# Four GNN layers on one core: layer 0's group boundary reordered, its evictions on two engines, one bias sum and one row transform moved

## The chip, the cores and the metric

The kernel runs on one core of a Trainium2 chip. The metric is the device time of one execution in microseconds (us); lower is better. Five engines work side by side, each through its own queue of instructions: TensorE (PE) multiplies matrices and writes PSUM, VectorE (DVE) and ScalarE (ACT) do elementwise work, GpSimd (POOL) does elementwise work on SBUF, and SyncE (SP) issues transfers. ACT and POOL issue transfers as well. Engines wait for each other by semaphores, which the tile framework sets.

## The reference, cut to what matters

There are N = 2708 nodes with 512 features, an int32 adjacency matrix of 0 and 1 (2708 x 2708), and four layers. Each is `x = x + layer(relu(layernorm(x)))`:

```python
# layer 0:  h = relu(layernorm(x))
out = (adj.T @ h) @ W0
x = x + relu(out * clip(adj.sum(axis=0), 1)[:, None] ** -0.5)
# layer 1:  keep = the first 64 neighbours of each row, by a running count along the row
x = x + leaky(h @ W_line.T + b_line) + leaky(mean(keep @ h) @ W_nb.T + b_nb)
# layer 2:  8 heads of graph attention, e = leaky(f1[:, None] + f2[None, :], 0.2), softmax over neighbours
x = x + elu(attention @ Wh)
# layer 3:  mean over neighbours and self, each through a weight, then both through W_comb
x = x + relu(concat(self, nb) @ W_comb + b_comb)
```

## The kernel before

Rows are cut into NC = 22 chunks of R = 126 (the last has 62), and chunks of columns into six groups of 4, 4, 4, 4, 3 and 3. Layer 0 multiplies by the weight first (`h0 = h @ W0`, split into two parts whose sum is exact enough, `halves`), then by the adjacency.

**Layer 0** (lines 350 to 462) runs over 132 units (group g, row chunk m). `staged` writes the steps of several units one behind the other: `load0` of unit i, the layer norm and product of chunk i (for the first 22 units alone), `count0` of unit i-3 and `multiply0` of unit i-4. This is the order of priority only. The framework's scheduler sets the final order within each engine's queue from a model of time, so an operation may stand some units ahead of its place.

- `load0` fetches a block of the adjacency (`ai`, three buffers).
- `count0`: VectorE casts it to `ar` for the products (line 381); ScalarE squares it into `ab`, a bf16 copy (line 383); VectorE scans along the row (line 388), which gives the running count `cum`; POOL keeps its last column in `deg` (line 396); ScalarE takes the sign of 64 minus the count, in place over `cum`, with the row sum into `signs` (line 397).
- `multiply0`: PE adds this unit's products to the group's 4 (or 3) accumulators (line 306), then transposes `ab` by multiplying with a unit matrix that has two columns of ones more (line 421), which also gives the column sums. ScalarE copies the transpose to `vT`, int8, which layers 1 to 3 read (line 424); VectorE takes the column sums out of the same PSUM tile (line 425). All PSUM tiles come from one pool of eight.
- After a group's last unit `finish0` sums the columns (line 439), takes 1/sqrt (lines 440 to 444), and for each chunk k of the group evicts the accumulator with relu and scale on ScalarE (line 449) into `y`, adds it to x on POOL (line 450), and writes x1 to memory, a transfer that the ScalarE queue issues (line 97). `y` and the layer norm's `hn` share three buffers (tag `t`).

**Ahead of layer 0** (lines 247 to 287) W_self and W_nb of layer 3 are each multiplied with their half of W_comb, and the biases too: eight matmuls with a broadcast bias column (line 279), then one addition on VectorE (line 286).

**Layer 2** first computes Wh = h W, f1 and f2 by chunk (lines 566 to 595). `row2` transposes f1 of a chunk to a row and copies it into `rows_T` (8 heads x 2772). After all chunks one Exp runs over `rows_T` (line 598), one transfer writes it to memory (`rT`, line 599), and each head's loop begins by loading its row, repeated on 126 partitions (`rb`, line 691). The loop scales it on ScalarE (`t`, line 702), combines it with the mask on VectorE (line 705) and multiplies on PE (line 715).

`load_x` (line 235) loads a chunk of x into a ring of seven buffers that all layers share. Weights of the layers take turns in two buffers (tag `w`).

Of the kernel before, what the change touches and what calls it, by code (L numbers as in the profile page):

```python
# [8 lines left out]
F32 = mybir.dt.float32  # L9
F32R = mybir.dt.float32r  # L10
BF16 = mybir.dt.bfloat16
I32 = mybir.dt.int32
# [30 lines left out]
def fast_layers(  # L43
# [188 lines left out]
            )  # L232
        return t

    def load_x(src, c, name="x", pool=None, bufs=7, twice=False):
        n = rows(c)
        t = (pool or common).tile([P, D], F32, name=name, bufs=bufs)
        if twice and c == NC - 1:
            nc.gpsimd.memset(t[:R], 0.0)
            move(nc.sync, t[TAIL : TAIL + n, :], src[c * R : c * R + n, :])  # L240
        move(nc.sync, t[:n], src[c * R : c * R + n, :])
        return t
# [4 lines left out]
    with tc.tile_pool(name="pre", bufs=2) as pre:  # L247
        ws = [load_weight(pre, w_self, "ws")]
        wc = load_weight(pre, w_comb, "wc", k=2 * NF)
        ws.append(load_weight(pre, w_nb3, "ws"))  # L250
        bc = load_row(pre, b_comb, "bc")
        bcol = pre.tile([P, 2 * NF], F32, name="bcol")
        for i, b in enumerate((b_self, b_nb3)):
            nc.sync.dma_start(
                bcol[:, i * NF : (i + 1) * NF], b.rearrange("(k p) -> p k", p=P)
            )
        for i in range(2):
            wsT = pre.tile([P, NF, D], F32, name="wsT")
            for f in range(NF):
                pt = ps.tile([P, NF, P], F32, name="wsT_ps", tag="ps")  # L260
                for k in range(NF):
                    nc.tensor.transpose(pt[:, k, :], ws[i][:, f, k * P : (k + 1) * P], ident)
                nc.scalar.copy(wsT[:, :, f * P : (f + 1) * P], pt)
            wf = pre.tile([P, NF, D], F32, name="wf")
            for f in range(NF):
                po = ps.tile([P, D], F32, name="fused_ps", tag="ps")
                for k in range(NF):
                    nc.tensor.matmul(
                        po,
                        wsT[:, k, f * P : (f + 1) * P],  # L270
                        wc[:, i * NF + k, :],
                        start=(k == 0),
                        stop=(k == NF - 1),
                    )
                nc.vector.tensor_copy(wf[:, f, :], po)
            nc.gpsimd.dma_start(fused[i].rearrange("(k p) o -> p k o", p=P), wf)
        pb = ps.tile([P, D], F32, name="bias3_ps", tag="ps")
        for k in range(2 * NF):
            nc.tensor.matmul(
                pb,  # L280
                bcol[:, k : k + 1].to_broadcast([P, P]),
                wc[:, k, :],
                start=(k == 0),
                stop=(k == 2 * NF - 1),
            )
        nc.vector.tensor_tensor(bc, pb, bc, ALU.add)
        nc.gpsimd.dma_start(bias3, bc[:1])

    vpool = ctx.enter_context(tc.tile_pool(name="vpool", bufs=1))
# [60 lines left out]
    with ExitStack() as ring_ctx:  # L350
        ring = ring_ctx.enter_context(tc.tile_pool(name="ring", bufs=NC - 1))

        w0s = load_weight(weights, w0, "w0s", tag="w")
        h0 = {}

        def product0(c, xc, hT, n):
            po = ps.tile([P, D], F32, name="h0_ps", tag="ps")
# [3 lines left out]
        with tc.tile_pool(name="l0", bufs=2) as wk:  # L361
# [2 lines left out]

            def load0(i):
                g, m = units[i]
                cs, n, gw = groups[g], rows(m), width(groups[g])
                ai = wk.tile([R, WG], I32, name="ai", bufs=3)
                block = adj[m * R : m * R + n, cs[0] * R : cs[0] * R + gw]
                if m == NC - 1:  # L370
                    nc.gpsimd.memset(ai[:, :gw], 0)
# [4 lines left out]
            def count0(i):  # L376
# [8 lines left out]
                if gw < KR:  # L385
# [21 lines left out]
            def multiply0(i):  # L407
# [4 lines left out]
                if m == 0:  # L412
                    for c in cs:
                        acc[c] = ps.tile([P, D], F32, name="acc", tag="ps")
                    sums[g] = wk.tile([R, KMAX, NC], F32, name="sums")
                for k, c in enumerate(cs):
                    matmuls(acc[c], h0[m], ar, k, m)

                pt = ps.tile([P, KMAX, P], F32, name="vT_ps", tag="ps")
                for k in range(K):  # L420
                    nc.tensor.matmul(
                        pt[:, k, :], ab[:n, k * R : k * R + P], ident1[:n], start=True, stop=True
                    )
                nc.scalar.copy(vT[g][:, :, m * R : (m + 1) * R], pt[:R, :K, :R])
                nc.vector.tensor_copy(
                    sums[g][:, :K, m : m + 1], pt[:R, :K, R : R + 1]
                )
                if m == NC // 2:
                    xs.update((c, load_x(x_in, c)) for c in cs)
                if m == NC - 1:  # L430
                    finish0(g)

            def finish0(g):
                cs = groups[g]
                K = len(cs)

                nc.gpsimd.memset(vT[g][:, :, N:], 1)
                nrm = small.tile([R, KMAX], F32, name="nrm")
                nc.vector.tensor_reduce(ind[:R, cs[0] : cs[-1] + 1], sums[g][:, :K], AX.X, ALU.add)
                nc.vector.tensor_scalar(  # L440
                    nrm[:, :K], ind[:R, cs[0] : cs[-1] + 1], 1.0, None, op0=ALU.max
                )
                nc.scalar.activation(nrm[:, :K], nrm[:, :K], AF.Sqrt)
                nc.vector.reciprocal(nrm[:, :K], nrm[:, :K])
                for k, c in enumerate(cs):
                    n = rows(c)
                    xc = xs.pop(c)
                    r = common.tile([P, D], F32, name="y", tag="t", bufs=3)
                    nc.scalar.activation(r[:n], acc.pop(c)[:n], AF.Relu, scale=nrm[:n, k : k + 1])
# [99 lines left out]
    with tc.tile_pool(name="l2", bufs=1) as cp:  # L549
# [13 lines left out]
        rows_T = pp.tile([H, NC * R], F32, name="rows_T", bufs=1)  # L563
        if N < NC * R:
            nc.gpsimd.memset(rows_T[:, N:], 0.0)
# [32 lines left out]
        nc.scalar.activation(rows_T[:, :N], rows_T[:, :N], AF.Exp, scale=1.0 - SLOPE2)  # L598
# [87 lines left out]
        for cs in spans:  # L686
            W = len(cs) * R
            for hd in range(H):
# [705 lines left out]
```

## Time and profile before

The time is 2215.93 us, the median of 3 runs (2213.86 to 2220.64). The profiled execution spans 2214.2 us. Its stages, by the lines that start in them and by the busy time of each engine in these stretches:

| stretch, us | what runs | PE busy | DVE busy | ACT busy | mean PE clock |
|---|---|---|---|---|---|
| 0 to 196 | fused weights, bias; dense part and group 0 of layer 0 | 178.62 | 90.70 | 75.89 | 0.98 |
| 196 to 248 | layer 0, group 1 | 49.16 | 34.87 | 37.22 | 0.96 |
| 248 to 308 | group 2 | 52.51 | 39.12 | 43.12 | 0.89 |
| 308 to 364 | group 3 | 49.77 | 37.62 | 41.07 | 0.94 |
| 364 to 413 | group 4 (3 chunks) | 39.40 | 30.43 | 34.86 | 0.90 |
| 413 to 458 | group 5 (3 chunks) | 39.65 | 30.59 | 32.59 | 0.89 |
| 560 to 760 | a part of layer 1 | 200.00 | 106.24 | 12.02 | 1.00 |
| 1000 to 1820 | layer 2, attention | 816.31 | 675.87 | 584.41 | 1.00 |
| 1820 to 2215 | layer 3 | 385.33 | 133.78 | 33.56 | 0.99 |

PE's busy time counts a matmul at half clock as busy too, so a stretch with a mean clock under 1 holds a second loss beside the idle time. The page's chain of waits names by line what ended last; the timeline lists instructions in order of time with the wait ahead of each, in square brackets, and what released it.

### The profile page before, as it was taken

The numbers are of one execution on the slowest core, as the hardware profiler recorded it, in microseconds if no ns is written. First come the engines' busy times: TensorE is split into PE (matmuls) and PEld (weight loads), VectorE is DVE, ScalarE is ACT, GpSimd is POOL, SyncE is SP. The second block draws the span as 40 slices with busy tenths as digits, with TensorE's granted clock in tenths as the row PEclk, the third lists the DMA queues.
The fourth block names the chain that finished last, engine by engine and source line by source line (L and its number), as shares of the span: only waits on it lengthen the run. The fifth ranks groups of instructions, "written<-read, shape, count | busy, mean of one in ns | idle before, by whom it ended". The sixth has DMA issues, their size and how long they took to land.

```text
span 2214.2 us, 21084 instructions
## 1 busy us (share of the span) xinstructions
PE 2116.3 (96%) x7176; PEld 1111.1 (50%) x7176; DVE 1379.4 (62%) x2137; ACT 972.4 (44%) x1489; POOL 244.2 (11%) x420
## 2 busy tenths in 40 slices
PE   8998888889999998879999999999999999999998
PEld 4555666644468875423333333333333334448886
DVE  4455666754446566658888888787888873323343
ACT  2445677741100001347777776666777762210000
POOL 1001232221102111310000000000001100000000
PEclk9999899999999999989999999999999999999999
DMA  6224444422221212010110201010100103211131
GB/s 236 70 75 125 131 139 125 114 81 71 71 77 52 62 43 93 31 45 25 25 33 26 60 28 28 28 28 24 35 25 24 31 9 93 67 57 57 57 106 34
DMA packets 117893, 140.64 MB, mean 64 GB/s; under 512 B 56784, under 2 KB 73404, under 8 KB 117768
## 3 DMA queue, kind: packets, MB, share of 16 engines
q1 hardware_dynamic: 80024, 103.82, 16.2%
q10 hardware_dynamic: 37176, 33.28, 4.8%
q0 software_dynamic: 576, 2.10, 0.3%
q8 instruction: 58, 0.95, 0.2%
q14 instruction: 59, 0.48, 0.1%
HBM read 103.54 MB, written 35.46 MB: 63 GB/s over the span
## 4 chain that ended last, share of the span: by engine, by line
PE 56%; ACT 1%; DMA 0%; DVE 0%; issue 0%; POOL 0%; DVEq 0%; ACTq 0%; SPq 0%
PE att L715 37%; PE acc L306 10%; PE nb_ps L165 3%; PE self_ps L165 3%; PE wh_ps L165 1%; ACT ot L649 1%; PE hT_ps L186 1%; PE out_ps L652 0%; DMA rb<-rT 0%; DMA rT<-rows_T 0%; DVE f L580 0%; ACT rows_T L598 0%; ACT t L702 0%; POOL wh_a L574 0%; DVE x L760 0%
## 5 line engine op out<-in xcount | busy, mean ns | idle before, releaser
L715 PE MATMUL att<-t,wh 126*65 126x504 f32 (+2 forms) x2112 | 828.5, 553 | 11.6 <-DVE t L705 11.6
L705 DVE SCALAR_TENSOR_TENSOR t<-t,eg,vT 126x882 f32<-126x882 f32 (+3 forms) x528 | 633.7, 1213 | 150.6 <-ACT t L702 149.1
L702 ACT ACTIVATE t<-rb,ef 126x882 f32<-126x882 f32 (+3 forms) x528 | 556.8, 1064 | 243.4 <-PE att L715 190.6
L715 PEld LDWEIGHTS att<-t,wh 126*65 126x65 f32 (+1 forms) x2112 | 287.7, 138 | 536.4 <-issue 449.5
L306 PE MATMUL acc<-halves,kt 126*126 126x512 f32 x1848 | 432.7, 395 | 1.2 <-DVE kt L522 1.2
L306 PEld LDWEIGHTS acc<-halves,kt 126*126 126x126 f32 x1848 | 343.8, 186 | 88.1 <-DVE kt L522 2.9
L306 PE MATMUL acc<-halves,ar 126*126 126x512 f32 x924 | 268.0, 431 | 22.2 <-DVE ar L381 12.9
L306 PEld LDWEIGHTS acc<-halves,ar 126*126 126x126 f32 x924 | 172.2, 197 | 72.2 <-DVE ar L381 14.5
L174 ACT ACTIVATE ln_rs<-ln_mv,eps 126x1 f32<-126x1 f32 x88 | 25.3, 293 | 319.5 <-DVE ln_mv L172 317.1
L522 DVE SCALAR_TENSOR_TENSOR kt<-lastr,index,vT 126x504 fp32r<-126x504 int16 (+1 forms) x132 | 104.3, 798 | 80.4 <-PE acc L306 79.7
L683 POOL TENSOR_TENSOR xs<-xs,e 126x448 f32<-126x448 f32 (+3 forms) x32 | 53.9, 1695 | 815.4 <-DVE e L669 815.4
L748 DVE CAST kt<-vT 126x504 fp32r<-126x504 int8 (+1 forms) x132 | 52.7, 400 | 144.8 <-PE acc L306 140.8
L388 DVE TENSOR_TENSOR_SCAN cum<-ai,deg 126x504 int16<-126x504 int32 (+2 forms) x110 | 125.9, 1146 | 25.7 <-DMA ai<-in_adj 15.4
L397 ACT ACTIVATE cum<-cum,limit 126x504 int16<-126x504 int16 (+3 forms) x132 | 88.1, 668 | 106.4 <-POOL ab L384 73.0
L188 ACT ACTIVATE hT<-hT_ps 128x504 f32<-128x504 f32 x88 | 51.1, 586 | 156.7 <-PE hT_ps L186 134.1
L170 DVE BATCH_NORM_STATS2 ln_st<-x 126x6 f32<-126x512 f32 x88 | 60.1, 686 | 85.0 <-DMA x<-x 65.4
L165 PE MATMUL wh_ps<-w2s,hT 128*126 128x512 f32 (+1 forms) x176 | 82.3, 611 | 7.8 <-ACT hT L188 7.8
L383 ACT ACTIVATE ab<-ai 126x504 bf16<-126x504 int32 (+3 forms) x132 | 76.7, 581 | 14.6 <-DMA ai<-in_adj 14.4
L165 PE MATMUL nb_ps<-wn,hT 128*126 128x512 f32 x176 | 81.5, 606 | 1.3 <-ACT hT L188 1.3
L165 PE MATMUL h_ps<-w0s,hT 128*126 128x512 f32 x176 | 79.3, 593 | 0.2 <-ACT hT L188 0.2
L165 PE MATMUL nb_ps<-wfn,hT 128*126 128x512 f32 x176 | 79.3, 593 | 0.2 <-ACT hT L188 0.2
L165 PE MATMUL line_ps<-wl,hT 128*126 128x512 f32 x176 | 79.1, 592 | 0.0
(132 smaller groups left out, 1503.8 us busy)
## 6 DMA issues: line engine op xcount, KB each, us to landing
x<-x SPq DMA_DIRECT2D x105, 252.0 KB
ai<-in_adj SPq DMA_DIRECT2D x84, 248.1 KB
x<-x ACTq DMA_DIRECT2D x63, 252.0 KB
x<-in_x SPq DMA_DIRECT2D x42, 252.0 KB
rb<-rT SPq DMA_DIRECT2D x16, 434.1 KB
s<-y ACTq DMA_DIRECT2D x21, 252.0 KB
sc<-s SPq DMA_DIRECT2D x21, 252.0 KB
out_x<-x ACTq DMA_DIRECT2D x21, 252.0 KB
```

What stands on the lines that cost most here:

```text
L165: nc.tensor.matmul(po[:n], lhsT[:, f, :n], w[:, f, :], start=(f == 0), stop=(f == NF - 1))
L170: nc.vector.bn_stats(st[:n], xc[:n])
L306: nc.tensor.matmul(acc[:R], weight[:, k * R : (k + 1) * R], parts[:, i, :], start=(m == 0 and i == 0), stop=(m == NC - 1),)
L383: nc.scalar.activation(ab[:n, :gw], ai[:n, :gw], AF.Square)
L388: nc.vector.tensor_tensor_scan(cum[:n, :gw], ai[:n, :gw], ai[:n, :gw], 0.0 if g == 0 else deg[:n, m : m + 1], op0=ALU.add, op1=ALU.max,)
L397: nc.scalar.activation(cum[:n, :gw], cum[:n, :gw], AF.Sign, bias=limit[:n], scale=-1.0, accum_out=signs[:n, m, g : g + 1],)
L522: nc.vector.scalar_tensor_tensor(by_chunk(kt, cs), lastr[:, cs[0] * R : (cs[-1] + 1) * R].rearrange("p (c r) -> p c r", r=R), index[:R, m ...
L683: nc.gpsimd.tensor_tensor(xs[:n, :q], xs[:n, :q], e[:n, k : k + q], ALU.add)
L702: nc.scalar.activation(t[:n, :W], rb[:n, :W], AF.Copy, scale=ef[:n, m, hd : hd + 1])
L705: nc.vector.scalar_tensor_tensor(by_chunk(t, cs)[:n], by_chunk(t, cs)[:n], eg[:n, m, hd : hd + 1], pattern(m, cs, n), op0=ALU.max, op1=ALU ...
L715: nc.tensor.matmul(a[:O1, : hi - lo], wh[:n, m, hd, :], t[:n, lo:hi], start=(m == 0), stop=(m == NC - 1),)
L748: nc.vector.tensor_copy(by_chunk(kt, cs), pattern(m, cs))
```

## The change

It has six parts. (1) In the last unit of a group the transposes and the column sums come ahead of the products, and the normalizing factor is computed before them. (2) Odd chunks are evicted on VectorE (`max` with 0, then times the factor), even ones on ScalarE as before. (3) The sign is written to a tile of its own (`sign`, bf16, one buffer), and in every unit the column sums (VectorE) stand ahead of the copy to `vT` (ScalarE). (4) `ai` has four buffers, and the x ring six. (5) The bias sum is formed on VectorE, by eight fused multiply-adds over 128 partitions, and one matmul with ones sums the partitions. (6) Layer 2's f1 row is written to memory by chunk from a small tile, the transfer issued by ScalarE, and the Exp moves to after the load of `rb`, on 126 partitions. The weights of layer 1 are asked for at unit 44 of layer 0, and not after it.

The purpose: the factor is to be ready when the products end, so that the accumulators are freed soon; the evictions are to share two engines; the sign need not wait until POOL has read the count; PE gets rid of seven bias matmuls; and the attention can start without one Exp and one transfer over all rows.

```diff
-    def load_x(src, c, name="x", pool=None, bufs=7, twice=False):
+    def load_x(src, c, name="x", pool=None, bufs=6, twice=False):
...
+        part = pre.tile([P, D], F32, name="part", bufs=1)
+        nc.vector.tensor_scalar(part, wc[:, 0, :], bcol[:, 0:1], None, op0=ALU.mult)
+        for k in range(1, 2 * NF):
+            nc.vector.scalar_tensor_tensor(
+                part, wc[:, k, :], bcol[:, k : k + 1], part, op0=ALU.mult, op1=ALU.add
+            )
         pb = ps.tile([P, D], F32, name="bias3_ps", tag="ps")
-        for k in range(2 * NF):
-            nc.tensor.matmul(
-                pb,
-                bcol[:, k : k + 1].to_broadcast([P, P]),
-                wc[:, k, :],
...
-        nc.vector.tensor_tensor(bc, pb, bc, ALU.add)
+        nc.tensor.matmul(pb[:1], ones, part, start=True, stop=True)
+        nc.vector.tensor_tensor(bc[:1], pb[:1], bc[:1], ALU.add)
...
+                if i == 2 * NC:
+                    l1_weights.extend(
+                        load_weight(weights, w, name, tag="w")
+                        for w, name in ((w_nb1T, "wn"), (w_line1T, "wl"))
+                    )
...
-                ai = wk.tile([R, WG], I32, name="ai", bufs=3)
+                ai = wk.tile([R, WG], I32, name="ai", bufs=4)
...
+                sign = wk.tile([R, WG], BF16, name="sign", bufs=1)
                 nc.scalar.activation(
-                    cum[:n, :gw],
+                    sign[:n, :gw],
                     cum[:n, :gw],
                     AF.Sign,
...
-                for k, c in enumerate(cs):
-                    matmuls(acc[c], h0[m], ar, k, m)
+                def products():
+                    for k, c in enumerate(cs):
+                        matmuls(acc[c], h0[m], ar, k, m)
+
+                if m < NC - 1:
+                    products()
 
                 pt = ps.tile([P, KMAX, P], F32, name="vT_ps", tag="ps")
                 for k in range(K):
                     nc.tensor.matmul(
                         pt[:, k, :], ab[:n, k * R : k * R + P], ident1[:n], start=True, stop=True
                     )
+                nc.vector.tensor_copy(sums[g][:, :K, m : m + 1], pt[:R, :K, R : R + 1])
+                if m == NC - 1:
+                    nrm = small.tile([R, KMAX], F32, name="nrm")
+                    total = ind[:R, cs[0] : cs[-1] + 1]
+                    nc.vector.tensor_reduce(total, sums[g][:, :K], AX.X, ALU.add)
+                    nc.vector.tensor_scalar(nrm[:, :K], total, 1.0, None, op0=ALU.max)
+                    nc.scalar.activation(nrm[:, :K], nrm[:, :K], AF.Sqrt)
+                    nc.vector.reciprocal(nrm[:, :K], nrm[:, :K])
+                    products()
                 nc.scalar.copy(vT[g][:, :, m * R : (m + 1) * R], pt[:R, :K, :R])
-                nc.vector.tensor_copy(
-                    sums[g][:, :K, m : m + 1], pt[:R, :K, R : R + 1]
-                )
...
-                    nc.scalar.activation(r[:n], acc.pop(c)[:n], AF.Relu, scale=nrm[:n, k : k + 1])
+                    if k % 2:
+                        nc.vector.tensor_scalar(
+                            r[:n],
+                            acc.pop(c)[:n],
+                            0.0,
+                            nrm[:n, k : k + 1],
+                            op0=ALU.max,
+                            op1=ALU.mult,
+                        )
+                    else:
+                        nc.scalar.activation(
+                            r[:n], acc.pop(c)[:n], AF.Relu, scale=nrm[:n, k : k + 1]
+                        )
...
-        wl = load_weight(weights, w_line1T, "wl", tag="w")
-        wn = load_weight(weights, w_nb1T, "wn", tag="w")
...
+        wn, wl = l1_weights
...
-            nc.tensor.transpose(pf[:H, :n], f12[:n, c, :H], ident[:n, :n])
-            nc.scalar.copy(rows_T[:, c * R : c * R + n], pf[:H, :n])
+            nc.tensor.transpose(pf[:H], f12[:R, c, :H], ident[:R, :R])
+            row = pp.tile([H, R], F32, name="row")
+            nc.scalar.copy(row, pf[:H])
+            nc.scalar.dma_start(rT[:, c * R : (c + 1) * R], row)
...
-        nc.scalar.activation(rows_T[:, :N], rows_T[:, :N], AF.Exp, scale=1.0 - SLOPE2)
-        nc.sync.dma_start(rT, rows_T)
...
+                nc.scalar.activation(rb[:, :W], rb[:, :W], AF.Exp, scale=1.0 - SLOPE2)
```

More of the change, by code (lines that the diff above doesn't have):

```diff
@@ L276, in fast_layers @@
             nc.gpsimd.dma_start(fused[i].rearrange("(k p) o -> p k o", p=P), wf)
-        pb = ps.tile([P, D], F32, name="bias3_ps", tag="ps")
-        for k in range(2 * NF):
-            nc.tensor.matmul(
-                pb,
-                bcol[:, k : k + 1].to_broadcast([P, P]),
-                wc[:, k, :],
-                start=(k == 0),
-                stop=(k == 2 * NF - 1),
-            )
-        nc.vector.tensor_tensor(bc, pb, bc, ALU.add)
+        part = pre.tile([P, D], F32, name="part", bufs=1)
[4 more added lines that the diff above has]
+            )
+        pb = ps.tile([P, D], F32, name="bias3_ps", tag="ps")
+        nc.tensor.matmul(pb[:1], ones, part, start=True, stop=True)
+        nc.vector.tensor_tensor(bc[:1], pb[:1], bc[:1], ALU.add)
         nc.gpsimd.dma_start(bias3, bc[:1])
@@ L354, in fast_layers @@
         h0 = {}
+        l1_weights = []
         def product0(c, xc, hT, n):
@@ L423, in multiply0 @@
                     )
+                nc.vector.tensor_copy(sums[g][:, :K, m : m + 1], pt[:R, :K, R : R + 1])
[7 more added lines that the diff above has]
+                    products()
                 nc.scalar.copy(vT[g][:, :, m * R : (m + 1) * R], pt[:R, :K, :R])
-                nc.vector.tensor_copy(
-                    sums[g][:, :K, m : m + 1], pt[:R, :K, R : R + 1]
-                )
                 if m == NC // 2:
                     xs.update((c, load_x(x_in, c)) for c in cs)
[L430 to L435, printed above, removed]
-                nc.gpsimd.memset(vT[g][:, :, N:], 1)
[L438 to L444, printed above, removed]
+                if m < NC - 1:
+                    return
+                nc.gpsimd.memset(vT[g][:, :, N:], 1)
                 for k, c in enumerate(cs):
@@ L562, in fast_layers @@
             )
-        rows_T = pp.tile([H, NC * R], F32, name="rows_T", bufs=1)
-        if N < NC * R:
-            nc.gpsimd.memset(rows_T[:, N:], 0.0)
         def product2(c, xc, hT, n):
```

## The prediction

> **What bounds the kernel now.** I read the page first: busy shares, then slices.
>
> ```profile
> PE 2116.3 (96%) x7176; PEld 1111.1 (50%) x7176; DVE 1379.4 (62%) x2137; ACT 972.4 (44%) x1489; POOL 244.2 (11%) x420
> ...
> PE   8998888889999998879999999999999999999998
> ...
> PEclk9999899999999999989999999999999999999999
> ```
>
> PE is the bound, busy for 96%. Work taken off another engine counts only where PE waits for it, and PE is idle for 2214.2 - 2116.3 = 97.9 us in all. The slices put the idle time in the first quarter (layer 0) and in slices 16 to 18 (layer 2's dense part and the entry to its attention); the attention has almost none. Next, PE's waits in 0 to 480 us (us in total, times, longest):
>
> ```profile
> PE acc L306 <- DVE ar L381: 13.6, 7, 3.9
> PE vT_ps L421 <- ACT ab L383: 13.2, 11, 2.1
> PE acc L306 <- DVE halves L227: 5.1, 8, 0.8
> ...
> PE acc L306 <- DVE sums L425: 4.2, 4, 2.1
> ...
> PE acc L306 <- DVE tail L230: 3.3, 1, 3.3
> ```
>
> Groups 1 to 5 own the first two rows. In an undisturbed stretch of the timeline a unit takes 2.155 us with 4 chunks, 1.634 with 3, so 22 units take about 46.7 and 35.5 us. The groups' first products stand at 196.5, 248.4, 308.3, 364.0 and 413.5, and the last transposes end at 457.9: they take 52.0, 59.9, 55.7, 49.5 and 44.4. The **boundary loss** is 5.3 + 13.2 + 9.0 + 14.0 + 8.9 = 50.4 us. The timeline from group 1 to group 2 shows how it arises (start, duration, engine, instruction, wait ahead of it):
>
> ```profile
> 247.78 0.39 PE L421 MATMUL vT_ps<-ident,ab 62*128 62x128 bf16 x4
> ...
> 251.86 0.56 ACT L424 CAST vT<-vT_ps 126x504 int8<-126x504 f32 x1
> ...
> 253.18 0.14 DVE L425 COPY sums<-vT_ps 126x4 f32<-126x4 f32 x1
> ...
> 254.07 0.18 DVE L444 RECIPROCAL nrm<-nrm 126x4 f32<-126x4 f32 x1 [0.27 <-ACT nrm L443]
> ...
> 254.64 1.82 ACT L449 ACTIVATE y<-acc,nrm 126x512 f32<-126x512 f32 x3
> ...
> 258.18 4.10 ACTq L97 DMA_DIRECT2D x<-x  x3
> ...
> 263.37 0.63 ACT L383 ACTIVATE ab<-ai 126x504 bf16<-126x504 int32 x1
> ...
> 264.06 0.40 PE L421 MATMUL vT_ps<-ident,ab 126*128 126x128 bf16 x4 [0.81 <-ACT ab L383]
> ...
> 269.70 1.22 PE L306 MATMUL acc<-halves,ar 126*126 126x512 f32 x2 [3.40 <-DVE ar L381]
> ```
>
> The last transposes end at 248.2, yet the first eviction starts at 254.64: sums wait for the copy to vT, which stands behind other work on ACT. Then ACT issues three stores, each waiting for a POOL addition, from 258.18 to 262.3, and only then does it make the next `ab`. PE, two units ahead, stops. The late squares free `ai` late, and the cast at 269.2 waits for a transfer.
>
> At the entry to layer 2 the chain of waits says:
>
> ```profile
> 963.69 2.36 ACT rows_T L598
> 966.07 2.86 DMA rT<-rows_T
> 969.07 4.49 DMA rb<-rT
> ```
>
> PE waits 11.6 us there. Lastly, eight bias matmuls hold PE for 7.03 us from 44.15 while everything behind them is ready.
>
> **What the Trainium skill says.** "TensorE: Matmul & The Clock Gate", Part 1: an idle window of some 3.4 us halves PE's clock until a busy window has passed. This trace agrees: the stretch table has PE's clock at 0.50 in 251.2 to 257.9 and 268.3 to 275.0, so a stop of 2 to 3 us costs up to 3.4 us more. The specification table at the head of that page gives ACT, DVE and POOL strict first-in-first-out queues; the trace agrees, the fourth eviction standing at 262.33 behind three stores. "DMA: Bandwidth & Descriptors", Anatomy of one DMA: a fixed cost of some 2.0 us, stated for transfers that GpSimd issues; here one from SyncE took 2.86 for 87 KB. "ScalarE: Activation LUTs", Table sets: exp and tanh share a set, sqrt is in another, so the moved Exp brings no table load inside the attention loop; the trace has a single 1.28 us load at this entry.
>
> **The change part by part.**
>
> *Bias.* PE loses seven of eight matmuls: 7.03 x 7/8 = 6.15 us, on the path. DVE gains eight operations of at most 0.69 us (line 508, same size), 5.5 us, ahead of 44 us; it was idle for 11.6 us before 13.78, and PE is held by the fused weights until 44. Cost 0, gain **6**.
>
> *Group 0.* The halves and tail waits (8.4 us) come from a loop: `ai` freed by a square, transfer (about 3 us), scan, sign, square. The sign no longer waits for POOL's read, 0.28 us a unit over some 11 units: **3**. The fourth `ai` buffer would open the loop (8 us) if the scheduler does not pull the scans one unit further ahead, which uses it up (0). I take 3.
>
> *Boundaries.* (a) Sums first and transposes ahead of products: the chain sums 0.14, sum 0.24, max 0.17, root 0.20, reciprocal 0.18 with its gaps is 1.1 us from sums to factor (253.18 to 254.25), beside last products of 0.9 to 1.1 us. First evictions, now 6.5, 5.0, 4.5 and 4.6 us after the last transposes (1.8 at the first boundary), can start within about 1 us. (b) Two of four evictions (0.69 each) leave ACT; DVE takes them at 0.7 each. The fourth no longer waits behind ACT's stores, which takes one eviction and its wait, about 1.7 us, off ACT's block. But **the stores stay on ACT**, and POOL's additions stay at 1.29 us (median): after the first eviction the last store still waits 3 or 4 additions, 3.9 to 6 us. So the block shrinks and isn't removed. (c) With four `ai` buffers the casts' wait, 1.76, 3.40, 2.13, 3.91 and 1.48, falls by up to one unit: 1.76 + 2.16 + 2.13 + 1.63 + 1.48 = 9.2 us at most. (d) Shorter stops spare half-clock windows, up to 3.4 us each. Against it: the copy to vT now waits for DVE, behind a 1.26 us scan; and DVE's second eviction waits for a `y` buffer, that is for an addition, with `ar` casts queued behind it and PE behind those. DVE has only 2.155 - 0.42 - 1.26 - 0.14 = 0.33 us spare a unit. Bounds: 0 (the wait moves to DVE) and 40 (only 10 of 50 stay). I take half of (c), 4.6, and 1.3 us a boundary for (a) and (b), 6.5, and two half-clock windows, 6.8: **18**.
>
> *Entry to layer 1.* `hn` shares buffers with the evictions: at 463.20 it waits for an addition. Last transposes end at 457.9, first eviction 460.83; with the factor early some **2** us.
>
> *Layer 2.* The chain loses an Exp of 2.36 and gains one of 1.04 (882 columns, as line 702). If `rb` still waits for the last row's store, 2.0 to 2.86 us, the gain is 1.3 to 2.2; if it needs only its own seven chunks, it starts when the work space is released, near 962.7, and the gain is 5.4. I take **3**. The 24 Exps on `rb`, 25 us, lie beside PE: ACT is busy for 584 of 820 us there and five `t` buffers decouple it. The 22 row stores cost ACT about 0.31 us each to issue. Where the dense part runs at 5.09 us a chunk (889 to 931) and not 3.97, the copy of hT follows the row copy at once, and PE follows hT; a store between them adds about 0.4 us to some nine chunks: 0 to 4, I take **-1.5**.
>
> *Nothing:* the x ring of six (a group needs four, and a chunk takes 4 to 7 us, a load some 3); layer 1's weights (`wl` came at 31.5 and `wn` at 189.3 already, as their buffers came free, so order alone changes).
>
> Sum: 6 + 3 + 18 + 2 + 3 - 1.5 = 30.5; 2215.9 - 30.5 = **2185**.
>
> **The rivals.** *Only the local gains* (0.17): the stores keep ACT blocked and the scheduler eats the `ai` buffer; bias 6 and layer 2's 3 remain: 2207. For it: at the boundary to group 5, with no fourth eviction, ACT still stood until 423.5. Against it: late evictions and transfer waits shrink on any order. *Boundaries mostly gone* (0.17): 40 there, 6 + 5 + 2 + 8 elsewhere: 2155. For it: half-clock windows vanish together with the stops; against it, the stores. *Slower* (0.11): DVE stands behind POOL at each boundary, 3 us more and a half-clock window at two, 15 + 6.8; row stores 4; less 6 + 2 + 6: the last 6 is what the earlier factor saves. 2216 + 25.8 - 14 = 2228. For it: 0.33 us of spare time; against it, `ar` has three buffers.
>
> **How the numbers follow.** The forecast has 0.55. The range leaves out the slower case and the far side of the large gain, about 0.2: 2155 to 2215. Within 0.3% means 2209.3 to 2222.6. Faster: 0.55 + 0.17 + some 0.10 of the local case (2207 lies near the limit) = 0.82; same 0.07; slower 0.11.
>
> **What would show it.** Right: one bias matmul and group 0's first product near 53 us in place of 59.3; the first eviction within about 1.5 us of the last products; waits for `ar` and `ab` under half of 26.8 us, and fewer stretches at half clock; no 87 KB store of rows ahead of `rb`, and the attention's first product about 3 us sooner after the last f1. Wrong: VectorE evictions that wait for POOL with casts behind them; ACT still idle for 4 us and more at its stores with PE stopped as before; chunks of layer 2's dense part at 5.5 us. What would upset everything is another order of the whole queue: the scheduler may move scans, sums and stores by units.

## The result, and the profile after

The changed kernel takes 2177.78 us (median of 4 runs, 2173.18 to 2178.70) against 2215.01 us on the same chip: a ratio of 0.9823, with a 95% interval of 0.9801 to 0.9845. The forecast was 2185 (2155 to 2215). But the sum hides two steps that were far too small and one loss that was not foreseen.

The page's busy shares and slices, after:

```profile
PE 2096.1 (96%) x7162; PEld 1101.0 (51%) x7162; DVE 1394.2 (64%) x2155; ACT 988.2 (45%) x1506; POOL 245.7 (11%) x419
...
PE   8999998899999989799999999999999999999998
...
PEclk9999999999999999999999999999999999999999
```

PE's idle time fell from 97.9 to 79.9 us (2176.0 - 2096.1), and its busy time by 20.2, of which the bias accounts for 6; most of the rest is the same work at a better clock. Of the eights in slices 4 to 9 (layer 0) two are left; the 7 at the entry to layer 2's attention stays.

PE's waits in 0 to 480 us (us in total, times, longest), after:

```profile
PE vT_ps L432 <- ACT ab L389: 10.9, 13, 2.0
...
PE acc L306 <- DVE ar L387: 3.9, 3, 2.3
```

The rows for `halves`, `tail` and `sums` (12.6 us before) no longer stand near the top. `ar` and `ab` together went from 26.8 to 14.8.

Stages between first and last matmuls of each kind, from the timeline of both profiles:

| stage | before | after | change | forecast |
|---|---|---|---|---|
| start to group 0's first product | 59.3 | 52.8 | -6.5 | -6 |
| group 0 | 136.7 | 123.6 | -13.1 | -3 |
| groups 1 to 5 | 261.9 | 238.0 | -23.9 | -18 |
| entry to layer 1 | 10.6 | 8.7 | -1.9 | -2 |
| layer 1 | 384.4 | 382.7 | -1.7 | 0 |
| layer 2, dense part | 97.5 | 100.0 | +2.5 | +1.5 |
| entry to the attention | 17.1 | 14.7 | -2.4 | -3 |
| attention | 848.2 | 856.9 | +8.7 | 0 |
| end of the attention to layer 3's last product | 381.4 | 381.4 | 0 | 0 |

Between the rows and at the ends 17.1 and 17.2 us are left out. These stages move by themselves too. In four kernels whose layer 0 is that of the changed one (after, and x4, x9 and x12 below) the start took 52.8 to 54.8 and groups 1 to 5 took 237.3 to 241.2. So a difference of 4 us in groups 1 to 5 says nothing by itself.

The boundary from group 1 to group 2 in the timeline (start, duration, engine, instruction, wait ahead of it), after:

```profile
228.70 1.19 PE L306 MATMUL acc<-tail,ar 126*126 126x512 f32 x4
...
231.46 0.24 DVE L439 TENSOR_REDUCE ind<-sums 126x4 f32<-126x88 f32 x1
...
232.38 0.18 DVE L442 RECIPROCAL nrm<-nrm 126x4 f32<-126x4 f32 x1 [0.27 <-ACT nrm L441]
232.60 0.75 DVE L456 TENSOR_SCALAR y<-acc,nrm 126x512 f32<-126x512 f32 x1
...
235.97 4.55 ACTq L97 DMA_DIRECT2D x<-x  x4
235.97 0.75 DVE L456 TENSOR_SCALAR y<-acc,nrm 126x512 f32<-126x512 f32 x1 [1.12 <-POOL x L468]
...
238.95 0.23 PE L432 MATMUL vT_ps<-ident,ab 126*128 126x128 bf16 x1 [1.35 <-POOL ab L390]
...
240.56 0.58 ACT L444 CAST vT<-vT_ps 126x504 int8<-126x504 f32 x1 [5.70 <-POOL ab L390]
...
242.89 0.28 PE L432 MATMUL vT_ps<-ident,ab 126*128 126x128 bf16 x2 [0.85 <-ACT ab L389]
```

The last products end at 229.9 and the first eviction starts at 232.60, so 2.7 us behind the group's last matmul and not 6.5. The factor is still late, since the reduction waits its turn on DVE. ACT stands at its four stores for 4.55 us, as the prediction said it would, and is idle for 5.70 us. Yet PE's longest stop here is 1.35 us, for GpSimd's clearing of `ab`, where it was 3.40 before; the stops between the last products and 243 us add up to 3.0 us, against 7.5 at this boundary before (247.8 to 270).

### The profile page after: what moved, and what is told of

Read it like the earlier page. It is cut to its first block, busy times and chain, and to the rows that moved or that the text cites. A ratio compares the mean times of both kernels' runs of the same rounds, so it can differ in the third digit from the quotient of the medians.

```text
span 2176.0 us, 21201 instructions
## 1 busy us (share of the span) xinstructions
PE 2096.1 (96%) x7162; PEld 1101.0 (51%) x7162; DVE 1394.2 (64%) x2155; ACT 988.2 (45%) x1506; POOL 245.7 (11%) x419
## 4 chain that ended last, share of the span: by engine, by line
PE 50%; ACT 3%; DMA 2%; DVE 2%; issue 1%; POOL 0%; SPq 0%; ACTq 0%; DVEq 0%; POOLq 0%
PE att L730 32%; PE acc L306 10%; PE nb_ps L165 3%; PE self_ps L165 3%; ACT t L717 2%; DMA rb<-rT 2%; DVE t L720 1%; PE out_ps L666 1%; ACT ot L663 1%; PE hT_ps L186 0%; DVE ln_st L170 0%; ACT rb L709 0%; POOL xs L697 0%; DVE x L775 0%; DVE hn L177 0%
## 5 line engine op out<-in xcount | busy, mean ns | idle before, releaser
L306 PE MATMUL acc<-halves,ar 126*126 126x512 f32 x924 | 254.9, 416 | 4.7 <-DVE ar L387 3.9
L306 PEld LDWEIGHTS acc<-halves,ar 126*126 126x126 f32 x924 | 166.1, 189 | 48.6 <-issue 7.0
L404 ACT ACTIVATE sign<-cum,limit 126x504 bf16<-126x504 int16 (+3 forms) x132 | 88.5, 670 | 69.3 <-DVE cum L394 62.2
L444 ACT CAST vT<-vT_ps 126x504 int8<-126x504 f32 (+1 forms) x132 | 70.7, 537 | 46.4 <-DVE sums L435 23.8
```

What stands on the lines that cost most here:

```text
L306: nc.tensor.matmul(acc[:R], weight[:, k * R : (k + 1) * R], parts[:, i, :], start=(m == 0 and i == 0), stop=(m == NC - 1),)
L404: nc.scalar.activation(sign[:n, :gw], cum[:n, :gw], AF.Sign, bias=limit[:n], scale=-1.0, accum_out=signs[:n, m, g : g + 1],)
```

## The experiments

Each was timed against the kernel before; ratios are given with their 95% interval. Layer 0 first.

**x1: three `ai` buffers.**

```diff
-                ai = wk.tile([R, WG], I32, name="ai", bufs=4)
+                ai = wk.tile([R, WG], I32, name="ai", bufs=3)
```

> The changed kernel (2177.8 us) with three ai buffers in layer 0 in place of four, nothing else. Theory A (the loop of ai freed by a square, transfer, scan, sign, square set group 0 and the casts' waits; the fourth buffer opened it): group 0's stalls come back, 8 us or more of its 123.4, and groups 1 to 5 lose another 5 to 9 of their 238.1: 2190 to 2197 us in all. Rival B (the sign's own tile, the start 6.5 us sooner and the new order opened group 0, the scheduler uses the fourth buffer up by pulling scans ahead): group 0 stays at 123 to 126 and the whole at 2176 to 2183.

2192.83 us, 0.9890 (0.9874 to 0.9907). Group 0 takes 124.0, groups 1 to 5 take 256.5, in a profiled run 3 us above the median. So theory A is right on the boundaries (18.5 us, twice what it said) and wrong on group 0, where rival B holds: the buffer does nothing there. That the whole fell into theory A's range is chance: it had split the loss otherwise. Busy times of groups 1 to 5 (stretch: length, then PE, PEld, DVE, ACT and POOL busy, PE's clock, DMA share, GB/s), one line each from before, after and x1:

```profile
196.00:457.90 261.90, 230.48 (x1174) 164.52 (x1174) 172.53 (x379) 188.77 (x461) 74.60 (x245) 0.91 0.45 128
```

```profile
176.40:414.40 238.00, 218.04 (x1172) 156.62 (x1172) 183.84 (x390) 183.27 (x451) 75.54 (x243) 0.99 0.49 141
```

```profile
177.80:434.30 256.50, 228.68 (x1173) 162.47 (x1172) 183.16 (x390) 185.59 (x453) 74.79 (x244) 0.94 0.47 132
```

The same matmuls take 230.48 us before, 218.04 after, 228.68 in x1. So of the 23.9 us gained, 12.4 are the clock and 11.5 are idle time (31.4 to 20.0). Of the buffer's 18.5, 10.6 are clock and 7.9 idle.

**x6: the kernel before with four `ai` buffers, x ring of six.**

```diff
-    def load_x(src, c, name="x", pool=None, bufs=7, twice=False):
+    def load_x(src, c, name="x", pool=None, bufs=6, twice=False):
...
-                ai = wk.tile([R, WG], I32, name="ai", bufs=3)
+                ai = wk.tile([R, WG], I32, name="ai", bufs=4)
```

> The kernel before with four ai buffers in layer 0 (and six x buffers, which pay for them), all else as before. Theory A (the fourth buffer alone is worth in groups 1 to 5 what three buffers cost the changed kernel, 18.5 us; nothing in group 0): groups 1 to 5 take 241 to 247 in place of 261.9, group 0 stays at 135 to 137, the whole at 2195 to 2202. Rival B (it is worth that only together with the evictions on two engines and the new order, since ScalarE stands at its stores anyway): groups 1 to 5 at 252 or more, 2206 and up.

2200.59 us, 0.9921 (0.9904 to 0.9937). Groups 1 to 5 take 247.2 in the profiled run, which at 2208.45 was 8 us above the median; group 0 takes 140.3. So it is theory A, at the edge of its range: four buffers, with the x ring of six, give about 15 us at the boundaries without any other part. They give nothing in group 0, which lies 3.6 us above its time before; why is not shown.

**x2: the order inside a unit as before** (sums behind the copy to vT, factor behind the products).

```diff
-                if m < NC - 1:
-                    products()
+                products()
...
-                nc.vector.tensor_copy(sums[g][:, :K, m : m + 1], pt[:R, :K, R : R + 1])
-                if m == NC - 1:
-                    nrm = small.tile([R, KMAX], F32, name="nrm")
...
-                    products()
                 nc.scalar.copy(vT[g][:, :, m * R : (m + 1) * R], pt[:R, :K, :R])
+                nc.vector.tensor_copy(sums[g][:, :K, m : m + 1], pt[:R, :K, R : R + 1])
...
                 nc.gpsimd.memset(vT[g][:, :, N:], 1)
+                nrm = small.tile([R, KMAX], F32, name="nrm")
...
```

> The changed kernel with the order inside a unit as before: products, transposes, copy to vT, sums; factor made after all of a group. Evictions on two engines, four ai buffers and the sign's tile stay. Theory A (early factor frees the accumulators sooner and is worth 1.3 us a boundary, as forecast): groups 1 to 5 take 244 to 249 in place of 238.1, the whole 2183 to 2189. Rival B (the order is worth more: it, not the buffer, made most of the 23 us gained at the boundaries): 253 or more, 2193 and up. Rival C (sums ahead of the copy to vT only move a wait from ACT to VectorE): 236 to 240, 2176 to 2181.

2191.27 us, 0.9888 (0.9868 to 0.9908). No theory had this: groups 1 to 5 stay at 235.2, as in rival C, and group 0 returns to 137.4. The whole gain of group 0 lies in the order, which the next run narrows down.

**x5: the kernel before with two statements swapped.**

```diff
-                nc.scalar.copy(vT[g][:, :, m * R : (m + 1) * R], pt[:R, :K, :R])
                 nc.vector.tensor_copy(
                     sums[g][:, :K, m : m + 1], pt[:R, :K, R : R + 1]
                 )
+                nc.scalar.copy(vT[g][:, :, m * R : (m + 1) * R], pt[:R, :K, :R])
```

> The kernel before with two lines swapped in layer 0: the copy of the neighbour sums stands ahead of the copy to vT; all else as before. Theory A (in group 0 the loop is load of ai, scan, sign, copies of vT and hT, square, next load, 7.05 us against TensorE's 5.97 a unit; the swap makes ScalarE do the square ahead of the copies of vT and hT and opens the loop by itself): group 0 takes 123 to 125 in place of 136.7, groups 1 to 5 stay within 4 of 261.9, the whole at 2200 to 2206. Rival B (it also needs the sign's own tile, or the earlier start): group 0 at 132 or more, the whole at 2211 or more. Rival C (the boundaries too come from VectorE waiting for ScalarE's copy to vT): groups 1 to 5 fall by 8 or more, 2190 to 2197.

2205.48 us, 0.9943 (0.9927 to 0.9960). Group 0 takes 123.9 in place of 136.7, groups 1 to 5 take 260.8: theory A, and the swap alone is all of group 0's gain. ACT's timeline in one unit of group 0, before:

```profile
102.87 0.71 ACT L397 ACTIVATE cum<-cum,limit 126x504 int16<-126x504 int16 x1 [4.15 <-POOL ab L384]
...
103.59 0.56 ACT L424 CAST vT<-vT_ps 126x504 int8<-126x504 f32 x1
104.05 0.59 ACT L188 ACTIVATE hT<-hT_ps 128x504 f32<-128x504 f32 x1
104.53 0.62 ACT L383 ACTIVATE ab<-ai 126x504 bf16<-126x504 int32 x1
```

and in x5:

```profile
100.09 0.71 ACT L397 ACTIVATE cum<-cum,limit 126x504 int16<-126x504 int16 x1 [2.58 <-POOL deg L396]
...
100.80 0.56 ACT L225 CAST halves<-h_ps 126x512 fp32r<-126x512 f32 x1
101.27 0.62 ACT L383 ACTIVATE ab<-ai 126x504 bf16<-126x504 int32 x1
102.53 0.58 ACT L427 CAST vT<-vT_ps 126x504 int8<-126x504 f32 x1 [0.64 <-DVE sums L424]
103.00 0.60 ACT L188 ACTIVATE hT<-hT_ps 128x504 f32<-128x504 f32 x1
```

The square on `ai` frees its buffer, and the next load is issued as it ends. Before, it started 1.66 us after the sign (102.87 to 104.53), behind the copies to vT and hT; in x5 it starts 1.18 us after. The load then takes 2.80 us from its issue to the scan and not 3.26; SyncE now issues it ahead of x's load and no longer behind it. In these stretches a turn of the loop (load, scan, sign, square) takes 7.05 us before (101.38 to 108.43 between two scans), and 6.1 to 6.3 in x5 and 5.93 in the changed kernel, where PE needs 5.97. A statement moved for VectorE's sake reordered ScalarE's queue.

**x10: the sign written back into `cum`.**

```diff
-                sign = wk.tile([R, WG], BF16, name="sign", bufs=1)
                 nc.scalar.activation(
-                    sign[:n, :gw],
+                    cum[:n, :gw],
```

> The changed kernel with the comparison written back into cum, as before, in place of its own tile. Theory A (the sign's wait for GpSimd's copy of deg is off every loop now that the square stands behind ScalarE's cast of halves and ahead of the copies of vT and hT): group 0 at 123.5 to 125, groups 1 to 5 within 3 of 238.0, the whole 2176 to 2182. Rival B (the wait, 0.28 us a unit as forecast, goes into the 5.93 us loop of group 0, which has only 0.04 us to spare): group 0 at 127 to 130. Rival C (in groups 1 to 5 GpSimd stands at its additions of 1.3 us, so that the sign waits for deg and the square behind it): groups 1 to 5 at 245 or more, 2185 and up.

2186.67 us, 0.9873 (0.9854 to 0.9893). Group 0 takes 126.7 (+3.1), groups 1 to 5 take 243.8 (2.6 above the scatter). Rival B on group 0, and C in part. ACT's waits in 180 to 440 us, x10:

```profile
ACT cum L403 <- POOL ab L390: 18.1, 12, 3.7
...
ACT cum L403 <- POOL deg L402: 12.6, 18, 2.7
```

The sign waits 30.7 us for POOL; the changed kernel has 4.0 us of that kind. In group 0 most units keep their 5.97 us: four take 6.07 to 7.06, and PE stops once for 1.5 us for `tail`.

**x7: all evictions on ScalarE.**

```diff
-                    if k % 2:
-                        nc.vector.tensor_scalar(
...
-                    else:
-                        nc.scalar.activation(
-                            r[:n], acc.pop(c)[:n], AF.Relu, scale=nrm[:n, k : k + 1]
-                        )
+                    nc.scalar.activation(
+                        r[:n], acc.pop(c)[:n], AF.Relu, scale=nrm[:n, k : k + 1]
+                    )
```

> The changed kernel with all of layer 0's evictions on ScalarE, all else as changed. Theory A (two evictions less on ScalarE and their place in its queue are worth 1 to 1.7 us a boundary, as the prediction had it): groups 1 to 5 take 243 to 247 in place of 238.0, the whole 2183 to 2187. Rival B (with the fourth ai buffer ahead of them, ScalarE's longer block is absorbed): within 3 of 238.0, 2176 to 2181. Rival C (VectorE is the tighter engine, with 0.33 us spare a unit, and gains from giving two evictions back): 230 to 235, 2170 to 2175.

2178.71 us, 0.9830 (0.9813 to 0.9847); groups 1 to 5 take 238.6. Rival B: the split of the evictions has no effect that can be measured.

**x8: the factor after the products, sums still ahead of vT; layer 2's rows as before.**

```diff
-                if m < NC - 1:
-                    products()
+                products()
...
-                if m == NC - 1:
-                    nrm = small.tile([R, KMAX], F32, name="nrm")
...
-                    products()
...
                 nc.gpsimd.memset(vT[g][:, :, N:], 1)
+                nrm = small.tile([R, KMAX], F32, name="nrm")
...
```

> The changed kernel with two parts undone: the factor after the last products as before (the sums stay ahead of the copy to vT), and layer 2's rows as before. Theory A (the order of sums and copy to vT alone opened group 0, and the early factor is worth nothing or costs up to 3 us): group 0 at 123 to 125, groups 1 to 5 at 234 to 238, attention at 848, the whole 2170 to 2174. Rival B (the early factor does its part once the sums stand first): groups 1 to 5 at 243 to 248, the whole 2178 to 2184. Rival C (what opened group 0 was the last unit's order): group 0 back at 136 to 138, 2184 to 2188.

2175.92 us, 0.9812 (0.9795 to 0.9828). Group 0 takes 124.0, so rival C is out. Groups 1 to 5 take 241.8; with x2's 235.2 on the other side of the scatter, the early factor can't be told from nothing there. It does show at the entry to layer 1: 10.1 to 10.6 us in the five profiles with a late factor (before, x2, x5, x6, x8), 8.7 to 9.2 in those with an early one and the stores on ScalarE.

**x3: x1's stores issued by GpSimd.**

```diff
-                    move(nc.scalar, x1[c * R : c * R + n, :], xc[:n])
+                    move(nc.gpsimd, x1[c * R : c * R + n, :], xc[:n])
```

> The changed kernel with layer 0's stores of x1 issued by GpSimd, right behind its own additions, in place of ScalarE. Theory A (at a boundary ScalarE still stands at its stores waiting for GpSimd's additions, and the 10.9 us for which TensorE waits for ab come from it): the wait for ab falls under 4 us, groups 1 to 5 take 226 to 232 in place of 238.1, the whole 2165 to 2172. Rival B (VectorE has only 0.33 us spare a unit and is the next limit; or the stores by GpSimd hold up its memsets of ab and its copies of deg): the wait moves to ar or stays, 2175 to 2182.

2179.24 us, 0.9825 (0.9809 to 0.9841). Groups 1 to 5 take 243.3, the entry to layer 1 takes 5.4 in place of 8.7. PE's waits in 0 to 480, x3:

```profile
PE vT_ps L432 <- POOL ab L390: 10.4, 4, 3.2
PE vT_ps L432 <- ACT ab L389: 8.5, 11, 1.6
```

Rival B: the wait for `ab` from ACT fell from 10.9 to 8.5 only, and that for POOL's clearing of `ab` went from 1.7 to 10.4.

**x11: the same, with that clearing in a group's first two units alone, in two fixed tiles, and layer 2's rows as before.**

```diff
+            abs2 = [wk.tile([R, WG + P - R], BF16, name=f"ab{j}", bufs=1) for j in range(2)]
...
-                ab = wk.tile([R, WG + P - R], BF16, name="ab")
+                ab = abs2[i % 2]
...
-                nc.gpsimd.memset(ab[:n, gw : KR + P - R], 0.0)
+                if m < 2:
+                    nc.gpsimd.memset(ab[:, gw : KR + P - R], 0.0)
...
-                    move(nc.scalar, x1[c * R : c * R + n, :], xc[:n])
+                    move(nc.gpsimd, x1[c * R : c * R + n, :], xc[:n])
```

> The changed kernel with layer 2's rows as before, layer 0's stores of x1 issued by GpSimd, and the pad of ab cleared in two fixed tiles at a group's first two units in place of by GpSimd in every unit. Theory A (with the stores on GpSimd the only new wait was TensorE's for the clearing of ab, 10.4 us, queued behind additions and stores; without it the boundaries shrink): groups 1 to 5 take 228 to 234 in place of 238.2, the whole 2162 to 2169. Rival B (what is left at the boundaries is the additions themselves and VectorE's 0.33 us spare a unit, so the wait moves to ar or to the vT copy): 236 to 243, 2170 to 2176.

2178.97 us, 0.9829 (0.9810 to 0.9848). Both theories miss: groups 1 to 5 rise to 251.2. PE now waits 25.9 us for ACT's `ab`, ACT 45.2 for the scan, and the scan 38.2 for `ai`'s load (7.4 in the changed kernel). In 230 to 430 us SyncE in turn waits 99.2 us for ACT's squares (61.2 in the changed kernel) before it issues; what slows this loop is not shown. So, with ScalarE free of stores groups 1 to 5 gained nothing, but in both runs another wait grew, and what the stores alone cost there stays open.

**x4: layer 2's rows as before.**

```diff
-            nc.tensor.transpose(pf[:H], f12[:R, c, :H], ident[:R, :R])
-            row = pp.tile([H, R], F32, name="row")
-            nc.scalar.copy(row, pf[:H])
-            nc.scalar.dma_start(rT[:, c * R : (c + 1) * R], row)
+            nc.tensor.transpose(pf[:H, :n], f12[:n, c, :H], ident[:n, :n])
+            nc.scalar.copy(rows_T[:, c * R : c * R + n], pf[:H, :n])
...
+        nc.scalar.activation(rows_T[:, :N], rows_T[:, :N], AF.Exp, scale=1.0 - SLOPE2)
+        nc.sync.dma_start(rT, rows_T)
...
-                nc.scalar.activation(rb[:, :W], rb[:, :W], AF.Exp, scale=1.0 - SLOPE2)
```

> The changed kernel with layer 2's part undone: rows gathered in rows_T, one Exp on them, one store, no Exp on rb inside the attention. Theory A (the attention's 8.6 us of loss come from the Exps on rb, which wait for rb's load in ScalarE's queue, and from four more table loads where layer 3's square roots fall between them): the attention takes 848 to 850 in place of 856.9, table loads fall from 10 to 6; the entry loses 2.3 and the dense part gains 2.4 again: 2168 to 2171. Rival B (the loss has another cause, such as the attention running at another time or other addresses): the attention stays at 855 to 858, the whole at 2176 to 2179.

2173.82 us, 0.9802 (0.9785 to 0.9818). The attention takes 847.8, the entry 17.0 again: theory A by stages, though the whole missed its 2168 to 2171. The dense part stays at 100.0, so the row stores did not cost the 2.5 us. This is the fastest kernel of the study. Its interval overlaps that of the changed kernel; by stages it gains 9.1 in the attention and gives back 2.3.

**x9: three `rb` buffers.**

```diff
-                rb = wk.tile([R, WM], F32, name="rb")
+                rb = wk.tile([R, WM], F32, name="rb", bufs=3)
```

> The changed kernel with three rb buffers in the attention in place of two, so that a head's rows are loaded one head sooner and the Exp on rb never waits for the load; the order of ScalarE's queue and its ten table loads stay. Theory A (two causes add up: the Exp's wait for rb's load, some 3 us over 24 heads, and the four more table loads with the stops they bring, some 6 us): the attention takes 853 to 855 in place of 856.9 (848.2 before), the Exp's wait for rb's load goes from 15.0 us to near 0, the whole 2174 to 2176. Rival B (all of it is the wait for the load): 848 to 850, 2169 to 2171. Rival C (all of it is table loads and the Exp's own 0.94 us): 856 to 857.5, 2177 to 2179.

2175.98 us, 0.9825 (0.9802 to 0.9848); attention 855.6. It doesn't tell the theories apart: the scheduler moved the Exp a head forward with the load, and it still waits 14.7 us for it (15.0 in the changed kernel).

**x12: layer 3's square roots kept out of the Exps.** Layer 3's norm reads its epsilon from a tile written after the sixth head of the last third.

```diff
+            if cs is spans[2] and hd == 5:
+                nc.vector.tensor_scalar(
+                    eps3[:R], e[:, 0, 0:1], 0.0, EPS, op0=ALU.mult, op1=ALU.add
+                )
...
-        staged(NC, *dense(x3, product3))
+        staged(NC, *dense(x3, product3, eps=eps3))
```

> The changed kernel, rows by chunk and the 24 Exps on rb kept, but layer 3's normalizations read a constant that is written only after the sixth head of the attention's last third, so that none of their square roots falls among the Exps of the middle third; table loads fall from 10 to 6. Theory A (the table loads where square roots fall between the Exps made 6.7 of the 8.7 us that the attention lost, the Exps' own waits the other 2): the first three heads of the middle third take 38.3 to 38.8 in place of 40.0 to 40.9, the attention 849.5 to 851.5 in place of 856.9, the whole 2169 to 2173. Rival B (the Exps on rb and their waits for its load slow those heads, with or without table loads): the attention 855 to 857, the whole 2175 to 2179. Rival C (the stop moves to where the square roots now fall): the three heads at 38.5, but heads of the last third at 35 or more, the whole 2174 to 2178.

2175.48 us, 0.9820 (0.9804 to 0.9837). In the attention the times of theory A came: 850.1, the three heads at 38.0, 38.5 and 38.5, no loss in the last third. The whole missed its 2169 to 2173; in the profiled run start and groups 1 to 5 (54.7 and 241.2) took 5.1 us more than in the changed kernel, at the slow end of their scatter. What x12 took away, in ACT's timeline of the changed kernel:

```profile
1237.81 1.28 ACT L709 ACT_TABLE_LOAD   x1
1239.10 1.04 ACT L709 ACTIVATE rb<-rb 126x1008 f32<-126x1008 f32 x1
...
1244.19 1.28 ACT L174 ACT_TABLE_LOAD   x1
1245.48 0.29 ACT L174 ACTIVATE ln_rs<-ln_mv,eps 126x1 f32<-126x1 f32 x1
...
1248.29 1.28 ACT L680 ACT_TABLE_LOAD   x1
```

PE's stops in the same heads, in the changed kernel:

```profile
1201.73 0.77 PE L666 MATMUL out_ps<-ident,ot 65*126 65x65 f32 x7 [0.78 <-ACT ot L663]
...
1243.19 0.50 PE L666 MATMUL out_ps<-ident,ot 65*126 65x65 f32 x4 [1.04 <-ACT ot L663]
...
1284.06 0.47 PE L666 MATMUL out_ps<-ident,ot 65*126 65x65 f32 x4 [1.00 <-ACT ot L663]
```

Three heads take 39.96, 40.91 and 40.88 us, against 38.15, 38.45 and 38.45 before: 6.7 us. The mean clock in 1196 to 1286 was 0.95, and 1.00 in x12's same heads. Theory A's sum came, but its split doesn't hold for the first of these heads. Half clock begins there at 1202.5, behind the stop of 0.78 us, and the first table load of this third comes at 1222.29. Ahead of that stop ACT shows an Exp that waited for its load, with two `t`s and then the copies to `ot` behind it:

```profile
1198.12 1.04 ACT L709 ACTIVATE rb<-rb 126x1008 f32<-126x1008 f32 x1 [0.58 <-DMA rb<-rT]
1199.07 2.14 ACT L717 ACTIVATE t<-rb,ef 126x1008 f32<-126x1008 f32 x2
1201.12 0.93 ACT L663 COPY ot<-att 65x504 f32<-65x504 f32 x2
```

So 4.9 us go with the table loads, in the second and third head, and the 1.8 of the first with the Exp and the clock. In x12 the stop at this place is 0.59 us and no half clock follows.

## Why the prediction was right, and where it was not

- **Bias, 6.** Right: one matmul pair takes 1.02 us where 7.03 stood, and group 0 starts 6.5 us sooner.
- **Group 0, 3.** The loop was named rightly and its terms were mis-sized. The fourth buffer's lower end, 0, was the true one (x1). The sign's tile costs 3.1 us to take away (x10). The size is the one priced, but by luck: not 0.28 us in each of some 11 units, but a few longer units and one stop of 1.5 us. The failed step is "Against it: the copy to vT now waits for DVE", which took this order as a cost. It moved the square ahead of two copies and gave 12.8 us by itself (x5). The parts don't add: x5 reaches 123.9 without the sign's tile; why the changed kernel needs the tile was not settled.
- **Boundaries, 18.** 23.9 came. Waits were forecast at 4.6 + 6.5 = 11.1, and idle time fell by 11.5, but from other terms. (a) and (b), 6.5, brought nothing that can be measured (x2, x7, x8). (c), the buffer, brought 7.9 in place of 4.6 by idle time alone. (d), "two half-clock windows, 6.8", brought 12.4: six stretches at half clock reach into these groups before, and two after. The rest of the idle time was not split up; the order of sums isn't it (x5: 260.8). "The stores stay on ACT" was seen rightly, but to move them brought nothing here (x3, x11).
- **Entry to layer 1, 2.** Right, 1.9, and by the early factor (x2, x8).
- **Layer 2, entry 3, row stores -1.5.** The entry gave 2.4, inside 1.3 to 5.4. The dense part lost 2.5, near the 1.5 by luck, as the row stores aren't the cause (x4). All profiles with an x ring of seven (before, x5) take 97.5 to 97.7, and those with six 98.5 to 100.2. The spacing of 5.09 us a chunk begins one chunk sooner in all of these, x6 and x4 with the old rows among them. Without the first spacing, which moves between 5.35 and 7.02 us, the stage takes 91.5 us before and 93.0 to 93.2 in x6, x4 and the changed kernel. So the failed step is "Nothing: the x ring of six", about 1.6 us; the ring was not changed alone.
- **24 Exps, 0.** The step that failed most, by 8.7 us. The forecast counted ACT's busy time and forgot its order. The Exp waits for a load with `t`s queued behind it: about 2 us remain in x12 (850.1 against 848.2), and 1.8 more came with the half clock of one head. And square roots of layer 3, which the scheduler had hoisted into the attention already before, now alternate with Exps (4.9 us). The Trainium skill's "ScalarE: Activation LUTs", Table sets, says that exp and sqrt lie in different sets and that one should batch by set. The trace agrees, with ten loads of 1.28 us where six were before. The prediction read the page rightly and looked at the loop's source rather than at ACT's queue in the trace, where a table load for line 174 stood inside the attention before the change, at 1264.7 us.
- **Layer 1, 0.** It gained 1.7 us in its aggregation. 1.2 of it is one wait of PE for VectorE's `kt`, which is gone after; no run here says why.

Of its signs, the first product came at 52.8 as said, and the clock rose. The first eviction of groups 0 to 5 starts 0.58, 2.70, 1.79, 0.52, 1.51 and 0.33 us after the last products, so two of six miss the 1.5. `ar` and `ab` stayed just over half of 26.8. Of the signs of being wrong, a VectorE eviction did wait for POOL with casts behind it, once, for 1.12 us (at 235.97), and ACT did stand at its stores, but PE did not stop as before. The sum came near because errors of both signs met: 10.1 and 5.9 too little at group 0 and the boundaries, against 8.7 in the attention.

## What to carry to other kernels

When two engines read one result, the order of the two statements can decide which queue stands still, as it did here; follow what lies behind each, up to the operation that frees a buffer. A function of another table set that the scheduler had hoisted cost little here alone (no stop of PE over 0.28 us between those heads before) and 4.9 us once Exps alternated with it, so read the queue in the trace, not the loop in the source. A buffer more, which decouples a load from short stops, was worth 7.9 us of idle time here and 10.6 more in the clock.

## What was not expected of the hardware

A stop of 0.78 to 1.04 us can be followed by half clock: in the changed kernel the clock is at 0.50 for 3.41 us from 1202.5, 1243.5 and 1284.5, right behind the stops of 0.78, 1.04 and 1.00 us. One of them, as a stretch of its own (columns as above):

```profile
1243.50:1246.90 3.40, 3.40 (x8) 0.98 (x7) 3.06 (x8) 2.25 (x3) 0.00 (x0) 0.50 0.00 0
```

In x10, with the same ten table loads, the heads have stops of 0.72, 0.36, 1.04 and 0.98 us and only one such stretch, behind the last of them, and they take 38.46, 39.22 and 40.86 us in place of 39.96, 40.91 and 40.88. The 3.2 us between the sums are about 1.6 for each of the two stretches fewer. So what the table loads cost depends on whether half clock follows.

All stretches at half clock in both profiles, but for the one that the end cuts off, last a multiple of 3.41 us, and within a profile they begin on one grid of this step. "TensorE: Matmul & The Clock Gate", Part 1, of the Trainium skill speaks of an idle window of some 3.4 us, and the prediction took the trace before as agreeing. No window of the grid need be idle here. Before, from 12 us to the last product, each of the ten windows at full clock that half clock follows has PE busy for 0.39 to 1.66 of its 3.41 us (1.66 ahead of 251.1), and each of the others for 1.76 or more. After, it is not so clean: a window with 1.57 (from 185.4) is not followed by half clock, and those with 2.64, 2.21 and 2.42 ahead of the attention's three stretches are. What decides there is open.
